# Slot attention and FP8 FFN on one core: where the output projection's products stand among a unit's other products

## The chip, the cores and the metric

The kernel runs on one core of a Trainium2 chip. Its time is the device time in microseconds (us) of that core; the number compared is the median of several runs. TensorE (PE in the profile, its weight loads PEld) multiplies, VectorE (DVE), ScalarE (ACT) and GpSimd (POOL) work on the products, and SyncE (SP) issues most of the DMAs.

## The reference: what is computed

Four sequences of 512 tokens with 512 features go through one layer. After a layer norm, attention with 16 heads and 64 slots per head reads and writes running states; after a second layer norm there is a feed-forward part whose weights are rounded to FP8. Cut to the attention (the recurrences run over the tokens):

```python
q, k, v, s = heads of h @ Wq, h @ Wk, h @ Wv, clip(h @ Ws, -32, 32)     # 64, 64, 128, 64 wide
z = cumlogsumexp(s);  g = exp(z_prev - z);  p = exp(s - z)
hk = hk * g + k (x) p;   ok = q . hk                # scores of the 64 slots
pv = softmax(ok)                                    # weights of the slots
hv = hv * g + p (x) v;   ov = pv . hv               # the read-out, 128 wide
o = ov * rsqrt(mean(ov**2) + eps) * g_norm * silu(h @ Wg)
x = x + o @ Wo                                      # the output projection
x = x + ffn(layernorm(x))
```

## The kernel before, in words

The 16 heads are taken two at a time (8 groups `g`) and the four sequences `b` in two pairs, which gives 32 units (g, b). Groups alternate: an even group also computes the values of the next odd one, so its unit is longer. Within a unit the 512 tokens stand in 4 blocks `n` of 128. The recurrences are turned into products: inside a block with a triangular mask (`diagonal_blocks`), and between blocks with sums of states (`states`, `add_up`).

The order of all engines is written out by hand: instructions stand on each engine's queue in the order in which Python calls them, and each engine works in that order. `attention` (L952) writes out one unit. It computes the unit X and, woven into it, the end of the unit before (`before`): normalising, gating, and the output projection `project_output` (L861), 4 blocks. A block's projection is six 128x512 products: four into the sum `ps_o` (parts 0 and 1 of the operands, two heads each) and two into `ps_o_m` (part 2). ACT then copies `ps_o` to `y` (L879), and `add_output` (L882) lets DVE subtract `ps_o_m` (L884) and POOL issue a DMA that adds `y` to the stream in DRAM (L885).

The second half of a unit, in which the change lies, runs thus on PE (L1051 to L1084):

- `slot_scores` ends with products into `ps_ok` (L731); DVE multiplies them into `okT` (L739).
- `value_states`: products into `ps_sv` (L636), which DVE adds up.
- `softmax`: four transposes of `okT` into `ps_okn` (L604); DVE takes the maxima `mx` (L746) and subtracts them (`ok`, L748); `softmax_exp` lets ACT take the exponential (L753).
- the projections of blocks 0 and 1.
- `slot_weights`: four transposes of `ok` into `ps_w`; DVE scales them into `wT` (L770).
- the projections of blocks 2 and 3; block 2's `ps_o_m` takes one of three shared banks, all other sums take turns in three "proj" banks.
- `weight_slot`: products of `eT` and `wT` into `ps_b` (L622); DVE masks them into two tiles `b` (L626), one for each head.
- `read_out`: products of `wT` with the states (L784), then of `b` with the values (L793), all into `ps_ov`; ACT squares, DVE reduces to `rs` (L804, L805), POOL takes the power (L808).

Two products of this stretch have row groups of their own: L622 and L784 use 64 rows each (64\*128 in the profile), two heads at a time; most others use 128 (128\*128).

The next unit then begins with 12 products each for s, k and q (L528, L551); DVE finishes `eT`, scales the output of the unit before (`og`, L813), runs the sum `z` (L688) and finishes `kT` (L555). `eT` is then transposed (`ps_e`), and `kT` (`ps_kn`), with the transposes of `og` (`ps_oT`) before it in odd groups.

Besides, a list `work` holds small pieces that have nothing to do with the unit at hand: splitting the weights of the groups to come (`w_...`, L256 on ACT, L263 to L268 on DVE) in the first 16 units, layer norms (`stats`, `mv`, `rstd`, `xn`, L342 to L349; `xs`, L378, L380), and rounding the FFN weights (`q`, `qw`, L471 to L485) in the last 16. `other`, `piece`, `small` take such pieces from the list at fixed places: between `softmax` and the projection of block 0 (L1054 to L1059), between the projections of blocks 2 and 3 (L1070), before `read_out` (L1076 to L1083), and in the next unit. `next_step` writes the transposes of a layer norm. `need("o")` empties the list up to the weights of the projection.

Of the kernel before, what the change touches and what calls it, by code (L numbers as in the profile page):

```python
# [37 lines left out]
F32 = mybir.dt.float32  # L38
# [6 lines left out]
P = 128  # L45
# [4 lines left out]
def kernel(  # L50
# [18 lines left out]
    nc = tc.nc  # L69

    B, T, D = x.shape
# [6 lines left out]
    HG = 2  # L78
# [15 lines left out]
    ps3 = ctx.enter_context(tc.tile_pool(name="ps3", bufs=3, space=bass.MemoryType.PSUM))  # L94
# [15 lines left out]
    def bank(name, n=None):  # L110
        if n is None:
            n = turn[0]
            turn[0] = (n + 1) % 3
        if n in held:
            held.pop(n)()
        return ps1.tile([P, 512], F32, tag=f"bank{n}", name=name)
# [47 lines left out]
    wt = {}  # L164
    split = {}
    work = []
# [3 lines left out]
    def other(count=None):  # L170
        for _ in range(count or pace[0]):
            if work:
                work.pop(0)[1]()

    def piece():

        while work:
            name, run = work.pop(0)
            run()
            if not name.endswith("_") and run is not scale_low:  # L180
                break

    def need(key):

        while any(name == key for name, _ in work):
            other(1)
# [4 lines left out]
    for g in range(NG):  # L191
# [3 lines left out]
        for nm in names:  # L195
            n = g if nm != "v" else 0 if g == 0 else (g + 1) // 2
# [5 lines left out]
    def fetch():  # L202
        if to_fetch:
            nm, g, part, chunks = to_fetch.pop(0)
            src, width = MATRICES[nm]
            tag = f"raw{fetched[0] % 2}"
            fetched[0] += 1
            w = one.tile([P, RAW], F32, tag=tag, name=f"raw_{nm}_{g}_{part}")[:, : chunks * width]
            if nm == "o":
                rows = src[g * HV : (g + 1) * HV, :]  # L210
            else:
                rows = src[part * chunks * P : (part + 1) * chunks * P, g * width : (g + 1) * width]
            nc.sync.dma_start(
                w.rearrange("p (c n) -> p c n", c=chunks), rows.rearrange("(c p) n -> p c n", p=P)
            )
            raw.setdefault((nm, g), []).append(w)
# [72 lines left out]
    def turned():  # L289

        return bool(work) and work[0][0][:3] == "xs_"

    def next_step():
        if steps:
            steps.pop(0)()
# [221 lines left out]
    class Projection:  # L517


        def __init__(self, nm, b, col0, name):  # L520
            self.nm, self.b, self.col0, self.name = nm, b, col0, name
# [131 lines left out]
    class Heads:  # L653


        def __init__(self, g, b):
            self.u, self.g, self.b = f"{g}_{b}", g, b
            self.v0 = g % 2 * HV
            self.sg = []
            self.y = {}  # L660

        def slots(self):

# [108 lines left out]
        def weight_slot(self):  # L772
            self.bb = diagonal_blocks(self.eT, self.wT, f"b_{self.u}")

        def read_out(self):


            po = [
                ps2.tile([P, NT, DV], F32, tag="acc", name=f"ps_ov_{self.u}_{h}") for h in range(HG)
            ]  # L780
            for n in range(1, NT):
                for h in range(HG):
                    rows = slice(h * M, (h + 1) * M)
                    nc.tensor.matmul(  # L784
                        po[h][:, n, :],
                        self.wT[rows, n * P : (n + 1) * P],
                        self.sv[rows, n - 1, :],
                        start=(n == 1),
                        stop=False,
                    )  # L790
            for h in range(HG):
                for n in range(NT):
                    nc.tensor.matmul(  # L793
                        po[h][:, n, :],
                        self.bb[h][:, n, :],
                        both_v[self.b][:, n, self.v0 + h * DV : self.v0 + (h + 1) * DV],
                        start=False,
                        stop=(n == NT - 1),
                    )
            self.og = one.tile([P, HG, NT, DV], F32, tag="og", name=f"og_{self.u}")  # L800
            rs = two.tile([P, HG, NT], F32, tag="rs", name=f"rs_{self.u}")
            for h in range(HG):
                nc.scalar.activation(self.og[:, h], po[h], AF.Square)  # L803
                nc.vector.tensor_reduce(rs[:, h, :], self.og[:, h], AX.X, ALU.add)  # L804
            nc.vector.scalar_tensor_tensor(  # L805
                rs, rs, 1.0 / DV, self.sm.rearrange("p (n h) -> p h n", h=HG), ALU.mult, ALU.add
            )
            nc.gpsimd.tensor_tensor(rs, rs, mhalf.rearrange("p (h n) -> p h n", h=HG), ALU.pow)  # L808
            self.po, self.rs = po, rs

        def scale_output(self):

# [45 lines left out]
            lo = self.oT[:, 1, h, :]  # L858
            nc.scalar.mul(lo, lo.bitcast(F32), 1.0 / DELTA)

        def project_output(self, n, in_bank=False):  # L861

            name = f"ps_o_{self.u}_{n}"
            p = ps3.tile([P, D], F32, tag="proj", name=name)
            m = bank(name + "_m") if in_bank else ps3.tile([P, D], F32, tag="proj", name=name + "_m")
            for dst, which in ((p, (0, 1)), (m, (2,))):
                for i in which:
                    for h in range(HG):
                        nc.tensor.matmul(  # L869
                            dst,  # L870
                            self.oT[:, i, h, n * P : (n + 1) * P],
                            wt["o"][:, i, h * D : (h + 1) * D],
                            start=(i == which[0] and h == 0),
                            stop=(i == which[-1] and h == HG - 1),
                        )
            if n == 0:
                self.y_all = one.tile([P, NT, D], F32, tag="y", name=f"y_{self.u}")
            y = self.y_all[:, n, :]
            nc.scalar.mul(y, p, 1.0 + DELTA)  # L879
            self.y[n] = y, m  # L880
# [6 lines left out]
    def exp_and_log():  # L887
        nc.scalar.preload_act_table_set("natural_log_exp_and_others")

    def first_unit():  # L890


        X = Heads(0, 0)

        parts = layernorm(0, 1, first=lambda: X.values(0))
        for nm in "skqv":
            load_matrix(nm, 0, True)
        for item in [item for item in work if item[0] in ("s_", "k_", "q_")]:
            work.remove(item)
            item[1]()  # L900
        X.values(1)
        for _ in range(5):
            piece()
        transposing = layernorm(1, 1)
        work.extend(parts())
        load_matrix("g", 0, True)
        other(2)
        X.slots()
        other(2)
        X.keys(X.running_sum)  # L910
        other(2)
        X.queries(None)
        X.turn_e()
        X.turn_k()
        other(2)
        X.values(2)
        other(2)
        X.key_states()
        X.inverse()
        X.values(3)  # L920
        fetch()
        fetch()
        load_matrix("o", 0, True)
        other(1)
        transposing()
        next_step()
        other(2)
        X.query_key()
        next_step()
        other(3)  # L930
        X.gate_main(0)
        X.slot_scores()
        X.value_states()
        next_step()
        X.softmax()
        X.softmax_exp()
        other(1)
        X.gate_main(1)
        X.slot_weights()
        next_step()  # L940
        X.gate_silu(0)
        X.gate_silu(1)
        exp_and_log()
        X.weight_slot()
        need("xs_1")
        X.softmax_sum()
        need("xs_0")
        piece()
        X.read_out()
        return X  # L950

    def attention(g, b, before, load, gated):  # L952
# [3 lines left out]
        X = Heads(g, b)  # L956
# [93 lines left out]
        exp_and_log()  # L1050
        X.slot_scores()  # L1051
        X.value_states()
        X.softmax()
        if even and b == 1 and not first and not turned():  # L1054
            piece()
        elif not turned():
            small()
        elif not even and b > 1:
            other(1)  # L1059
        need("o")  # L1060
        before.project_output(0)
        X.softmax_exp()
        before.add_output(0)
        before.project_output(1)
        X.slot_weights()
        before.add_output(1)
        next_step()
        before.project_output(2, True)
        before.add_output(2)
        small()  # L1070
        before.project_output(3)
        load("o")
        X.weight_slot()
        before.add_output(3)
        X.softmax_sum()
        if even and b == 1 and not first and not turned():  # L1076
# [3 lines left out]
        if even:  # L1080
            next_step()
            if turned():
                other(1)  # L1083
        X.read_out()  # L1084
        if not even and b < 2:
            next_step()
            if turned():
# [97 lines left out]
    with tc.manual_schedule(engines=EVERY):  # L1185
# [13 lines left out]
        before = first_unit()  # L1199
# [3 lines left out]
        for i, (g, b) in enumerate(units[1:], 1):  # L1203
# [53 lines left out]
            before = attention(g, b, before, load, gated)  # L1257
# [11 lines left out]
        for b in range(B):  # L1269
            need(f"xs_{b}")  # L1270
            for c in range(NFC):
                if c > 1:
                    other(2)
                h = ffn_hidden(b, c)
# [74 lines left out]
```

## Time and profile before

| | |
|---|---|
| median of 3 runs | 1456.88 us (1455.47 to 1457.69) |
| span of the profiled execution | 1454.5 us |
| mean granted TensorE clock | 0.999 |
| PE, busy | 1429.6 us (98%), 8875 matmuls |
| PEld, busy | 1178.9 us (81%) |
| DVE, busy | 1104.0 us (76%) |
| ACT, POOL, busy | 709.9 us (49%), 240.0 us (16%) |
| chain that ended last | PE 89%, DVE 7%, ACT 2%, issue 1% |

The profile's own execution spans 1454.5 us from its first to its last instruction; the median of the runs is 2.4 us above that. Rows of a timeline read: start, duration of the merged group, engine, line, operation, written tile <- read tiles, shape, count, and in brackets the idle time of the engine before the group with what ended it. PE's ends are modelled and overlap the next start, so the distance from start to start is the better measure.

### The profile page before, as it was taken

Reading aid. Unit: us, or ns where it says so; the run is one execution under the profiler, and the core shown is the slowest. Engines: PE = TensorE matmul, PEld = TensorE weight load, DVE = VectorE, ACT = ScalarE, POOL = GpSimd, SP = SyncE. Lnnn points to the kernel's source line nnn. Section 1 sums busy time; section 2 is a strip of 40 time slices with the busy share of each in tenths; the row PEclk is TensorE's granted clock in tenths of the full one; section 3 lists DMA queues with packets and bytes.
Section 4 is the critical chain, followed back from the end, with each engine's and each line's share of the span. In section 5 each row is a group of like instructions: output and inputs, shape, how many; then the busy total and the mean of one; then the engine's idle time right before and its main releaser. Section 6 shows DMA issues by size and latency. Waiting matters only on the chain.

```text
span 1454.5 us, 22772 instructions
## 1 busy us (share of the span) xinstructions
PE 1429.6 (98%) x8875; PEld 1178.9 (81%) x8875; DVE 1104.0 (76%) x1968; ACT 709.9 (49%) x1215; POOL 240.0 (16%) x271
## 2 busy tenths in 40 slices
PE   9999999999999999999999999999999999999998
PEld 4778888888888888888888888888888788888886
DVE  6888868976897689878888898898889863435333
ACT  4555555555665556554545554556445542222221
POOL 2012111211121122211211121111112111000000
PEclk9999999999999999999999999999999999999999
DMA  8274556565655474456546654666465562101000
GB/s 333 86 218 138 182 160 172 175 191 158 174 174 185 135 232 123 138 156 192 160 109 196 203 161 108 196 203 173 127 179 174 145 181 30 59 0 58 1 29 29
DMA packets 80859, 212.51 MB, mean 146 GB/s; under 512 B 6168, under 2 KB 35120, under 8 KB 75568
## 3 DMA queue, kind: packets, MB, share of 16 engines
q1 hardware_dynamic: 62224, 177.49, 33.1%
q0 software_dynamic: 18528, 33.58, 15.2%
q8 instruction: 70, 1.15, 0.3%
q14 instruction: 37, 0.30, 0.1%
HBM read 107.23 MB, written 108.00 MB: 148 GB/s over the span
## 4 chain that ended last, share of the span: by engine, by line
PE 89%; DVE 7%; ACT 2%; issue 1%; POOL 0%; DMA 0%; DVEq 0%; POOLq 0%
PE ps_o L869 8%; PE ps_g L528 8%; PE ps_v L587 7%; PE ps_fg L1097 6%; PE ps_fu L1097 6%; PE ps_ov L793 4%; PE ps_o_m L869 4%; PE ps_g_m L551 4%; PE ps_v_m L587 4%; PE ps_s L528 3%; PE ps_k L528 3%; PE ps_q L528 3%; PE ps_fd L1158 3%; PE ps_fe L1158 3%; PE ps_b L622 2%; PE ps_a L622 2%
## 5 line engine op out<-in xcount | busy, mean ns | idle before, releaser
L885 POOL DMA_DIRECT2D stream<-y x128 | 112.4, 884 | 476.3 <-DVE y L884 468.6
L869 PE MATMUL ps_o<-w_o,oT 128*128 128x512 f32 x512 | 145.2, 405 | 0.0
L528 PE MATMUL ps_g<-xs,w_g 128*128 128x512 f32 x496 | 125.2, 394 | 0.0
L587 PE MATMUL ps_v<-w_v,xs 128*128 128x512 f32 x480 | 122.3, 397 | 0.2 <-DVE qT L555 0.2
L1118 DVE SCALAR_TENSOR_TENSOR h<-ps_fu,scol,act 128x512 f32<-128x512 f32 x48 | 36.0, 750 | 111.5 <-PE ps_fu L1097 110.2
L879 ACT ACTIVATE y<-ps_o 128x512 f32<-128x512 f32 x128 | 76.5, 598 | 74.9 <-PE ps_o L869 74.9
L528 PEld LDWEIGHTS ps_g<-xs,w_g 128*128 128x128 f32 x496 | 91.7, 188 | 19.7
L869 PEld LDWEIGHTS ps_o<-w_o,oT 128*128 128x128 f32 x512 | 91.4, 188 | 17.4
L587 PEld LDWEIGHTS ps_v<-w_v,xs 128*128 128x128 f32 x480 | 87.7, 188 | 19.4 <-DVE qT L555 0.6
L713 POOL COPY sk_both<-sk 64x192 f32<-64x192 f32 x64 | 43.5, 679 | 343.4 <-DVE sk L649 341.5
L1097 PE MATMUL ps_fg<-xs,wf 128*128 128x512 f32 x384 | 95.6, 391 | 0.0
L884 DVE TENSOR_TENSOR y<-y,ps_o_m 128x512 f32<-128x512 f32 x128 | 87.2, 681 | 10.4 <-ACT y L879 9.8
L1097 PE MATMUL ps_fu<-xs,wf 128*128 128x512 f32 x384 | 94.8, 389 | 0.0
L595 ACT ACTIVATE v<-ps_v 128x512 f32<-128x512 f32 x60 | 35.9, 599 | 99.9 <-PE ps_v L587 99.9
L803 ACT ACTIVATE og<-ps_ov 128x512 f32<-128x512 f32 x64 | 38.1, 597 | 94.5 <-PE ps_ov L793 94.5
L1097 PEld LDWEIGHTS ps_fu<-xs,wf 128*128 128x128 f32 x384 | 72.1, 188 | 15.0
L1097 PEld LDWEIGHTS ps_fg<-xs,wf 128*128 128x128 f32 x384 | 71.6, 188 | 14.6
L869 PE MATMUL ps_o_m<-w_o,oT 128*128 128x512 f32 x256 | 79.4, 391 | 0.2 <-ACT y L879 0.2
L596 DVE TENSOR_TENSOR v<-v,ps_v_m 128x512 f32<-128x512 f32 x60 | 41.0, 684 | 48.6 <-PE ps_v_m L587 48.6
L1124 ACT CAST both<-h 128x512 fp32r<-128x512 f32 x48 | 29.8, 621 | 94.5 <-DVE h L1118 94.5
L1115 ACT ACTIVATE act<-ps_fg,scol 128x512 f32<-128x512 f32 x48 | 33.0, 688 | 87.7 <-PE ps_fg L1097 87.7
L533 ACT ACTIVATE sg<-ps_g 128x512 f32<-128x512 f32 x62 | 37.0, 596 | 71.4 <-PE ps_g L528 44.4
(171 smaller groups left out, 3327.0 us busy)
## 6 DMA issues: line engine op xcount, KB each, us to landing
stream<-y POOLq DMA_DIRECT2D x128, 256.0 KB, 6.3
split_v<-w_v SPq DMA_DIRECT2D x4, 3072.0 KB, 12.3
split_g<-w_g SPq DMA_DIRECT2D x8, 1536.0 KB, 7.6
split_o<-w_o SPq DMA_DIRECT2D x8, 1536.0 KB, 6.3
w_v<-split_v SPq DMA_DIRECT2D x4, 3072.0 KB, 16.3
w_g<-split_g SPq DMA_DIRECT2D x8, 1536.0 KB, 6.6
w_o<-split_o SPq DMA_DIRECT2D x8, 1536.0 KB, 9.5
rounded<-qw SPq DMA_DIRECT2D x36, 256.0 KB, 3.7
```

Source lines behind the costliest of these rows:

```text
L528: nc.tensor.matmul(self.p, products(self.nm, c, self.col0, i), xs[self.b][i][:, c, :], start=(i == 0 and c == 0), stop=(i == 1 and c == KC ...
L551: nc.tensor.matmul(self.m, products(self.nm, c, self.col0, 2), xs[self.b][2][:, c, :], start=(c == 0), stop=(c == KC - 1),)
L587: nc.tensor.matmul(dst, xs[b][i][:, c, n * P : (n + 1) * P], wt["v"][:, i, c * 2 * HV : (c + 1) * 2 * HV], start=(i == which[0] and c == 0 ...
L622: nc.tensor.matmul(pa[h][:, n, :], lT[rows, cols], rT[rows, cols], start=True, stop=True)
L713: nc.gpsimd.tensor_copy(sk_both[rows, :, h * M : (h + 1) * M], self.sk[rows])
L793: nc.tensor.matmul(po[h][:, n, :], self.bb[h][:, n, :], both_v[self.b][:, n, self.v0 + h * DV : self.v0 + (h + 1) * DV], start=False, stop ...
L869: nc.tensor.matmul(dst, self.oT[:, i, h, n * P : (n + 1) * P], wt["o"][:, i, h * D : (h + 1) * D], start=(i == which[0] and h == 0), stop= ...
L879: nc.scalar.mul(y, p, 1.0 + DELTA)
L884: nc.vector.tensor_tensor(y, y, m, ALU.subtract)
L885: nc.gpsimd.dma_start(stream[self.b][n * P : (n + 1) * P, :], y, accum_op=ALU.add)
L1097: nc.tensor.matmul(pp, w[:, c * P : (c + 1) * P], xs[b][k][:, c, :], start=(c == 0 and k == 0), stop=(c == KC - 1 and k == 1),)
L1158: nc.tensor.matmul(sums[n], parts[k][:, n * P : (n + 1) * P], fw[c][2], start=(c == 0 and k == 0), stop=(c == NFC - 1 and k == 1),)
```

## The change

The products of the projection get other places in the unit; what is computed stays. `project_output` can now emit a part of a block's six products (`count`) and go on later. `read_out` is cut in two: `read_states` (the products with the states) and `read_within` (the rest). In `attention`:

- two products of block 0 stand before the transposes of `softmax`, if no piece of the projection's weights is waiting;
- two products of block 2 stand before the transposes of `slot_weights`, its other four behind them;
- `weight_slot` stands before the projection of block 3, and that projection stands between `read_states` and `read_within`;
- the pieces of `work` that stood between `softmax` and block 0 stand behind `slot_weights`; the `small()` that stood between blocks 2 and 3 stands behind `weight_slot`.

```diff
-        def read_out(self):
+        def read_states(self):
-            po = [
+            self.po = po = [
...
+        def read_within(self):
+            po = self.po
...
-        def project_output(self, n, in_bank=False):
-            name = f"ps_o_{self.u}_{n}"
-            p = ps3.tile([P, D], F32, tag="proj", name=name)
-            m = bank(name + "_m") if in_bank else ps3.tile([P, D], F32, tag="proj", name=name + "_m")
-            for dst, which in ((p, (0, 1)), (m, (2,))):
...
+        def project_output(self, n, in_bank=False, count=None):
+            if n not in self.left:
+                name = f"ps_o_{self.u}_{n}"
+                p = ps3.tile([P, D], F32, tag="proj", name=name)
+                self.left[n] = [(p, i, h) for i in (0, 1) for h in range(HG)] + [
+                    (None, 2, h) for h in range(HG)
+                ]
+                self.sums[n] = [p, None]
+            p, m = self.sums[n]
+            for _ in range(count or len(self.left[n])):
+                dst, i, h = self.left[n].pop(0)
+                if dst is None:
+                    if m is None:
+                        name = f"ps_o_{self.u}_{n}_m"
+                        m = bank(name) if in_bank else ps3.tile([P, D], F32, tag="proj", name=name)
+                        self.sums[n][1] = m
+                    dst = m
+                nc.tensor.matmul(
+                    dst,
+                    self.oT[:, i, h, n * P : (n + 1) * P],
+                    wt["o"][:, i, h * D : (h + 1) * D],
+                    start=(i in (0, 2) and h == 0),
+                    stop=(i in (1, 2) and h == HG - 1),
+                )
+            if self.left[n]:
+                return
...
         X.value_states()
+        if not any(name[0] == "o" for name, _ in work):
+            before.project_output(0, count=2)
         X.softmax()
+        need("o")
+        before.project_output(0)
+        X.softmax_exp()
+        before.add_output(0)
+        before.project_output(1)
+        before.project_output(2, count=2)
+        X.slot_weights()
         if even and b == 1 and not first and not turned():
             piece()
         elif not turned():
             small()
         elif not even and b > 1:
             other(1)
-        need("o")
-        before.project_output(0)
-        X.softmax_exp()
-        before.add_output(0)
-        before.project_output(1)
-        X.slot_weights()
         before.add_output(1)
         next_step()
         before.project_output(2, True)
         before.add_output(2)
+        X.weight_slot()
         small()
+        X.read_states()
         before.project_output(3)
         load("o")
-        X.weight_slot()
         before.add_output(3)
         X.softmax_sum()
...
-        X.read_out()
+        X.read_within()
```

The first unit has no unit before it and keeps its order, and the last unit's projection stands in the feed-forward part, whole blocks at a time.

More of the change, by code (lines that the diff above doesn't have):

```diff
@@ L659, in __init__ @@
             self.sg = []
-            self.y = {}
+            self.y, self.left, self.sums = {}, {}, {}
         def slots(self):
@@ L808, in read_out @@
             nc.gpsimd.tensor_tensor(rs, rs, mhalf.rearrange("p (h n) -> p h n", h=HG), ALU.pow)
-            self.po, self.rs = po, rs
+            self.rs = rs
         def scale_output(self):
@@ L859, in low_output @@
             nc.scalar.mul(lo, lo.bitcast(F32), 1.0 / DELTA)
-        def project_output(self, n, in_bank=False):
-            name = f"ps_o_{self.u}_{n}"
-            p = ps3.tile([P, D], F32, tag="proj", name=name)
-            m = bank(name + "_m") if in_bank else ps3.tile([P, D], F32, tag="proj", name=name + "_m")
-            for dst, which in ((p, (0, 1)), (m, (2,))):
[L867 to L875, printed above, removed]
+        def project_output(self, n, in_bank=False, count=None):
[24 more added lines that the diff above has]
+                return
             if n == 0:
@@ L1069, in attention @@
         before.add_output(2)
+        X.weight_slot()
         small()
+        X.read_states()
         before.project_output(3)
         load("o")
-        X.weight_slot()
         before.add_output(3)
@@ L1083, in attention @@
                 other(1)
-        X.read_out()
+        X.read_within()
         if not even and b < 2:
```

## The prediction

> **What bounds the kernel now.** First the page: PE is busy 98% and carries 89% of the chain, so the time is PE's products plus what PE waits for.
>
> ```profile
> PE 1429.6 (98%) x8875; PEld 1178.9 (81%) x8875; DVE 1104.0 (76%) x1968; ACT 709.9 (49%) x1215; POOL 240.0 (16%) x271
> ...
> PE 89%; DVE 7%; ACT 2%; issue 1%; POOL 0%; DMA 0%; DVEq 0%; POOLq 0%
> ```
>
> Then the list of PE's waits. It hides the steady ones: it shows 1.5 us for `ps_okn`, but the view of that tile sums 14.8 us of idle (PE and PEld together) ended by `okT`, and the view of `ps_ov` 10.6 us ended by `b`. So the timeline has to be read, here of an odd unit, its PE and PEld, then its DVE.
>
> ```profile
> 436.17 1.09 PE L731 MATMUL ps_ok<-a,e 128*64 128x128 f32 x16
> 437.10 0.82 PE L636 MATMUL ps_sv<-v,e 128*64 128x128 f32 x12
> 438.06 0.66 PE L604 MATMUL ps_okn<-ident,okT 128*128 128x128 f32 x4
> 438.47 1.18 PE L869 MATMUL ps_o<-w_o,oT 128*128 128x512 f32 x4
> ...
> 441.33 0.60 PE L604 MATMUL ps_w<-ident,ok 128*128 128x128 f32 x4
> 441.73 1.19 PE L869 MATMUL ps_o<-w_o,oT 128*128 128x512 f32 x4
> 443.21 1.09 PE L869 MATMUL ps_o<-w_o,oT 128*128 128x512 f32 x4
> 444.69 1.16 PE L622 MATMUL ps_b<-wT,eT 64*128 64x128 f32 x16
> 445.68 0.84 PE L784 MATMUL ps_ov<-sv,wT 64*128 64x128 f32 x12
> 446.63 2.05 PE L793 MATMUL ps_ov<-v,b 128*128 128x128 f32 x16
> ```
>
> ```profile
> 438.06 0.42 PEld L604 LDWEIGHTS ps_okn<-ident,okT 128*128 128x128 f32 x4 [0.38 <-DVE okT L739]
> 446.62 0.74 PEld L793 LDWEIGHTS ps_ov<-v,b 128*128 128x128 f32 x6 [0.30 <-DVE b L626]
> ```
>
> See two waits per unit: the 12 records of `ps_sv` hold PE for 0.96 us up to `ps_okn`, where the 16 in front took 0.93; and the 12 of L784 for 0.95, up to L793. Both are ended by DVE, as PEld's brackets say, and both come in every unit but the first, 31 times. They are the places that the change fills. The same unit on DVE:
>
> ```profile
> 438.83 0.68 DVE L746 TENSOR_REDUCE mx<-ps_okn 128x8 f32<-128x512 f32 x1
> 440.15 0.68 DVE L263 TENSOR_TENSOR w_s<-raw_s,w_s 128x512 fp32r<-128x512 f32 x1
> 442.08 0.68 DVE L770 TENSOR_TENSOR wT<-ps_w,rzT 128x512 f32<-128x512 f32 x1
> 443.59 0.69 DVE L884 TENSOR_TENSOR y<-y,ps_o_m 128x512 f32<-128x512 f32 x1 [0.23 <-ACT y L879]
> 445.88 1.29 DVE L626 TENSOR_TENSOR b<-ps_b,tri 128x512 f32<-128x512 f32 x2 [0.27 <-PE ps_b L622]
> 449.35 0.69 DVE L804 TENSOR_REDUCE rs<-og 128x4 f32<-128x512 f32 x1 [0.19 <-ACT og L803]
> ```
>
> See that DVE has three short waits only from `mx` on: it is nearly full here, and what it has to do is fixed. The same queue must then deliver `kT` for the next unit's transposes. In a late unit the two stand so:
>
> ```profile
> 1076.47 0.68 DVE L555 TENSOR_TENSOR kT<-kT,ps_k_m 128x512 f32<-128x512 f32 x1
> ...
> 1077.70 0.60 PE L604 MATMUL ps_kn<-ident,kT 128*128 128x128 f32 x4
> ```
>
> `kT` ends at 1077.15, 0.55 us ahead of its reader.
>
> **PE's gain per unit.** No product is added; I lay the new order out from the start of `ps_sv`, 437.10. Rates from start to start: pairs of 64-wide products 0.11, twelve projection products behind transposes 2.86 (438.47 to 441.33), six 1.48, two 0.45, four transposes 0.36 unwaited. `ps_sv` takes 0.70; two products of block 0, with the entry behind 64-wide ones, 0.57: `ps_okn` at 438.37, after `okT` (437.31+0.69=438.00). Transposes to 438.73; twelve products to 441.59; `ps_w` to 441.95; four products 1.02 and the entry to 64-row ones 0.09: `ps_b` at 443.06. From there 0.99 (as 444.69 to 445.68), 0.76 for the states' six pairs and the way back to 128 rows, 1.49 for block 3: L793 at 446.30, and the next unit at 448.00 (0.10 less, since its first product does not wait) instead of 448.43. The gain is 0.43 us. Bounds: PE's own idle, 0.14+0.11=0.25, and PEld's, 0.38+0.30=0.68; I stay with the layout between them.
>
> The new waits in that layout. Block 2's first product takes the bank of block 0's `ps_o_m`, which DVE frees by the first `y` subtraction: `mx` 439.02 (0.19 later), `ok` 0.72 and `y` 0.61 later, done 441.02; the product's weights load 0.2 before its start at 441.14. Late by some 0.05: gain 0.40. `wT` can start 0.31 after the last transpose has (as `okT` does after the last `ps_ok`), 442.28 to 442.97, ahead of `ps_b` at 443.06 to 443.1. `b`: behind it DVE has the piece moved here (0.60, 0.72), `y`, `y` (0.61, 0.60), so `b` 445.41 to 446.10 against 446.30. Three margins of 0.1 to 0.2 us; below them 0.1 more lateness costs 0.1 a unit. ACT is in time: `y` of block 0 can start at 439.4 now that the `w_s` copy (0.63) no longer precedes it, and is done 0.3 before DVE wants it.
>
> The two split blocks add borders between transposes and products. Row: `ps_w` starts 0.45 after two products begin, products 0.40 after the transposes, no dearer than inside a group; I price a border at nothing (upper bound 0.02). [...]
>
> **What the moved pieces cost.** DVE used the time in which it now waits for `ps_w` for a piece. In the unit above, the queue has done the same list 1.50 us later (`wT` 0.18 later and 1.32 of piece behind it), less the waits that close, 0.23+0.27+0.19: 0.8 us late at `rs` and, the queue being full up to it, at `kT`, while PE comes 0.40 earlier. `ps_kn` then waits 0.8+0.40+0.05 (the first transpose's extra, 329 against 273 ns) less its slack. In the late unit pieces L478, L479 are shorter (1.06), the lateness 0.76, the slack 0.55: wait 0.7, unit 0.3 slower. Where DVE waits for POOL's `rs` before `og`, closing the wait before `eT` gives nothing. The slack `kT` to `ps_kn`, the closing waits and the piece, read so in every unit (numbered from 0):
>
> - 12 units keep 0.40: without a piece here (4, 8, 12, 16), with slack 1.96 (7, 11), with wide waits before `b` or `eT` (17, 18, 21, 26, 29), and the last, 31: 4.8 us.
> - 3 and 15: `okn` waits 0.6 longer, two whole products fit: 0.63 each, 1.3.
> - 6, 10, 20, 22 to 25, 27: slack 0.5 to 1.07, 0.08 to 0.24 left: 1.2.
> - 5, 9, 13, 19, 28: slack 0.55 to 0.94, lateness 0.8 to 0.9: -0.31, -0.33, -0.07, -0.31, -0.35: -1.4.
> - 1, 2, 14, 30 already wait at `ps_kn` (up to 1.15 us) for a chain that starts at `rs`: PE's gain is lost and DVE's shift remains. 1 has no piece before `wT`, `rs` comes 0.7 earlier: +0.7. 2: 0.8 late; 30: 1.51 less 0.67, 0.84 late; 14, without any wait to close, 1.55 late: -3.2.
>
> Sum: 4.8+1.3+1.2-1.4+0.7-3.2 = 3.4 us faster. Against the profiled execution: span 1454.5 to 1451.1; the median lies 2.4 above, 1453.5.
>
> At nothing I price: the split DMAs and raw loads of the moved pieces, which go on SP 2.5 us later (they land in 3.1 to 6.5 us; the `w_q` load of the unit above is wanted 5.5 us after its new issue; a late one would hold a later piece, 1 us in some of the nine units that have such a piece here); `load("o")` 1.7 us later (lands in 9.5, read 30 us on); POOL's stream DMA of block 3, about 1 us later and still 1 us ahead of POOL's power; k's bank, freed by block 3's `y` at 448.7 and wanted at 450.9. Each cover that fails puts its own lateness on PE once a unit.
>
> **The rivals.**
> 1. *The lateness is absorbed.* If `kT` is not later, each unit keeps 0.40, 12.4 us and 0.5 at 3 and 15: 1444. For it: DVE idles 24% overall. Against: not one wait between `rs` and `kT` in the late units.
> 2. *The waits before `b` do not close (slower).* If DVE, now reaching `y` and `b` in another order, still waits 0.7 there, the lateness is 1.5 instead of 0.8. Price: 0.7 in nine units (5, 6, 9, 10, 13, 19, 22, 25, 28) and about 0.4 in eight more, 9.5 us in all: 1463; half of it 1458. It decides from 0.25 us of extra lateness a unit, which eats the 3.4. For it: the margins above. Against: both blocks' sums are complete before DVE arrives.
> 3. *The waits only move.* Blocks 0 and 2 wait for their bank as long as `okn` did: the unit keeps 0.14 of the 0.40. The sum then reads 1.7+0.8+0.9-1.4+0.7-3.2 = 0.5 us slower, 1457.4. For it: block 2 starts 0.05 us from its bank's release. Against: a wait of 0.26 there needs DVE 0.2 later than its rows.
>
> **Chances and range.** Forecast 0.55 (1450 to 1456.5), rival 1 0.12, rival 2 0.23, rival 3 0.10. The range reaches towards 1 and to half of 2: 1446.5 to 1459.5. About 0.2% (2.9 us) is what a measurement can tell from no change: faster 0.36+0.12 = 0.48, same 0.19+0.10 = 0.29, slower 0.23.
>
> **What would show it.** `ps_sv` to the first product 0.70, no PEld idle before `ps_okn` and L793, 448.0 instead of 448.4 within the unit; DVE idle 1.2 us before `wT`, none before `b`; and PE waits for `kT` at `ps_kn` in about 13 more units, 0.1 to 0.7 us each. Wrong if L793 or `ps_b` waits for DVE in most units (slower), or if `ps_kn` never waits (1444).

## The result, and the profile after

The changed kernel takes 1458.04 us (median of 21 runs, 1456.78 to 1460.88), the kernel before 1456.22 (21 runs, 1455.06 to 1457.69). The ratio is 1.0015, with a 95% interval of 1.0009 to 1.0021: it is slower by 0.15%, where 0.2% faster was forecast. The profiled execution took 1456.78 us, its span is 1455.1, 0.6 longer than before's. Of the 21 runs it is the fastest; in twelve of the others the mean granted clock is lower than its 0.998 (0.994 to 0.997), and no profile shows where.

The page shows next to nothing of it (first its busy times, then the chain):

```profile
PE 1430.3 (98%) x8875; PEld 1176.3 (81%) x8875; DVE 1101.0 (76%) x1968; ACT 705.8 (49%) x1215; POOL 242.3 (17%) x271
...
PE 86%; DVE 7%; ACT 3%; issue 2%; POOL 1%; DMA 0%; SPq 0%; POOLq 0%; DVEq 0%
```

The list of PE's waits does (us in total, times, longest). Before, its line for `kT` read 2.1 us in 2, and it had no line for `ps_b` and `y`:

```profile
PE ps_kn L604 <- DVE kT L555: 4.7, 7, 1.8
PE ps_b L622 <- DVE y L900: 4.6, 2, 2.7
PE ps_xn L361 <- DVE xn L349: 4.6, 5, 2.1
...
PE ps_kn L604 <- DVE xs L378: 1.2, 2, 0.6
PE ps_oT L604 <- ACT e L700: 0.8, 4, 0.2
```

4.6 us in two waits is more than the whole gain that was forecast. They stand in units 14 and 30. First, though, the ordinary unit: the same one that the prediction reads, unit 11, on PE.

```profile
435.56 0.82 PE L636 MATMUL ps_sv<-v,e 128*64 128x128 f32 x12
436.31 0.73 PE L883 MATMUL ps_o<-w_o,oT 128*128 128x512 f32 x2
436.88 0.60 PE L604 MATMUL ps_okn<-ident,okT 128*128 128x128 f32 x4
437.23 0.71 PE L883 MATMUL ps_o<-w_o,oT 128*128 128x512 f32 x2
...
440.15 0.60 PE L604 MATMUL ps_w<-ident,ok 128*128 128x128 f32 x4
...
441.61 1.16 PE L622 MATMUL ps_b<-wT,eT 64*128 64x128 f32 x16
442.61 0.84 PE L784 MATMUL ps_ov<-sv,wT 64*128 64x128 f32 x12
...
444.87 1.95 PE L797 MATMUL ps_ov<-v,b 128*128 128x128 f32 x16
446.57 2.07 PE L528 MATMUL ps_s<-xs,w_s 128*128 128x512 f32 x8
```

From `ps_sv` to the next unit it now takes 446.57-435.56 = 11.01 us, where it took 448.43-437.10 = 11.33: 0.32 less. The waits before `ps_okn` and for `b` are closed, as the change was laid out. DVE in the same unit:

```profile
440.78 0.69 DVE L770 TENSOR_TENSOR wT<-ps_w,rzT 128x512 f32<-128x512 f32 x1 [1.26 <-PE ps_w L604]
...
443.91 1.28 DVE L626 TENSOR_TENSOR b<-ps_b,tri 128x512 f32<-128x512 f32 x2
...
453.56 0.66 DVE L555 TENSOR_TENSOR kT<-kT,ps_k_m 128x512 f32<-128x512 f32 x1
```

It idles 1.26 us before `wT`, not at all before `b`, and `kT` comes 18.00 us after the unit's `ps_sv` (453.56-435.56), where it came after 17.44 (454.54-437.10): 0.56 late. Before's row:

```profile
454.54 0.66 DVE L555 TENSOR_TENSOR kT<-kT,ps_k_m 128x512 f32<-128x512 f32 x1
```

In the late unit of the prediction, 28, the lateness is 0.63 (1075.38-1055.93 against 1076.47-1057.65), and there PE waits:

```profile
1076.11 0.66 PE L604 MATMUL ps_kn<-ident,kT 128*128 128x128 f32 x4 [0.31 <-DVE kT L555]
```

Now unit 14, PE:

```profile
552.72 0.60 PE L361 MATMUL ps_xn<-ident,xn 128*128 128x128 f32 x4
...
553.62 0.62 PE L883 MATMUL ps_o_m<-w_o,oT 128*128 128x512 f32 x2
554.17 0.48 PE L622 MATMUL ps_b<-wT,eT 64*128 64x128 f32 x2
557.34 1.04 PE L622 MATMUL ps_b<-wT,eT 64*128 64x128 f32 x13 [2.68 <-DVE y L900]
...
559.62 2.07 PE L883 MATMUL ps_o<-w_o,oT 128*128 128x512 f32 x4
```

and DVE:

```profile
553.52 0.68 DVE L342 BATCH_NORM_STATS2 stats<-x 128x6 f32<-128x512 f32 x1
...
554.98 0.68 DVE L900 TENSOR_TENSOR y<-y,ps_o_m 128x512 f32<-128x512 f32 x1
555.58 0.69 DVE L342 BATCH_NORM_STATS2 stats<-x 128x6 f32<-128x512 f32 x1
...
556.60 0.69 DVE L900 TENSOR_TENSOR y<-y,ps_o_m 128x512 f32<-128x512 f32 x1
```

In this unit the transposes `ps_xn` of a layer norm take one of the three shared banks. `ps_b` needs two, and the second one it gets is that of block 2's `ps_o_m`. Before, block 3 stood between block 2 and `ps_b`, so PE came 1.5 us later (six products). Now `ps_b` follows block 2 at once, and its third product waits until DVE has subtracted that very sum: the `y` at 556.60, queued behind a piece that was moved there and behind a second one (`stats`, `mv`, `rstd`) that stood there before too. Unit 30 is built alike (1.93 us). The same places before, on PE and on DVE:

```profile
556.00 0.62 PE L869 MATMUL ps_o_m<-w_o,oT 128*128 128x512 f32 x2
...
557.90 1.18 PE L622 MATMUL ps_b<-wT,eT 64*128 64x128 f32 x15
```

```profile
557.29 0.69 DVE L884 TENSOR_TENSOR y<-y,ps_o_m 128x512 f32<-128x512 f32 x1
```

Behind the changed kernel's wait, the table of the windows (start and end, length, busy time and instructions of PE, PEld, DVE, ACT, POOL; then the granted TensorE clock, the DMA share and GB/s):

```profile
554.70:557.30 2.60, 0.00 (x0) 0.00 (x0) 2.52 (x6) 0.00 (x0) 2.07 (x3) 1.00 0.20 34
557.40:558.40 1.00, 1.00 (x18) 1.00 (x20) 0.08 (x1) 0.00 (x0) 0.86 (x2) 1.00 1.13 80
558.50:561.80 3.30, 3.30 (x16) 2.69 (x14) 2.86 (x5) 0.07 (x1) 0.00 (x0) 0.50 0.91 132
```

The clock falls to half for these 3.3 us (3.41 by its records), and block 3's first four products span 1.87 us (559.62 to 561.49) where they took 1.04 in unit 11 (443.37 to 444.41).

### The profile page after: what moved, and what is told of

Read it like the earlier page. It is cut to its first block, busy times and chain, and to the rows that moved or that the text cites. A ratio compares the mean times of both kernels' runs of the same rounds, so it can differ in the third digit from the quotient of the medians.

```text
span 1455.1 us, 22778 instructions
## 1 busy us (share of the span) xinstructions
PE 1430.3 (98%) x8875; PEld 1176.3 (81%) x8875; DVE 1101.0 (76%) x1968; ACT 705.8 (49%) x1215; POOL 242.3 (17%) x271
## 3 DMA queue, kind: packets, MB, share of 16 engines
q8 instruction: 70, 1.15, 0.3%
## 4 chain that ended last, share of the span: by engine, by line
PE 86%; DVE 7%; ACT 3%; issue 2%; POOL 1%; DMA 0%; SPq 0%; POOLq 0%; DVEq 0%
PE ps_o L883 8%; PE ps_g L528 8%; PE ps_v L587 8%; PE ps_fg L1118 6%; PE ps_fu L1118 6%; PE ps_g_m L551 4%; PE ps_v_m L587 4%; PE ps_o_m L883 4%; PE ps_fd L1179 3%; PE ps_ov L797 3%; PE ps_fe L1179 3%; PE ps_s L528 3%; PE ps_k L528 3%; PE ps_q L528 2%; PE ps_a L622 2%; PE ps_ok L731 2%
## 5 line engine op out<-in xcount | busy, mean ns | idle before, releaser
L883 PE MATMUL ps_o<-w_o,oT 128*128 128x512 f32 x512 | 163.3, 421 | 0.0
L883 PEld LDWEIGHTS ps_o<-w_o,oT 128*128 128x128 f32 x512 | 84.8, 190 | 25.2 <-DVE y L900 7.0
L812 POOL TENSOR_TENSOR rs<-rs,mhalf 128x8 f32<-128x8 f32 x32 | 58.8, 1839 | 78.8 <-DVE rs L809 54.6
```

Source lines behind the costliest of these rows:

```text
L883: nc.tensor.matmul(dst, self.oT[:, i, h, n * P : (n + 1) * P], wt["o"][:, i, h * D : (h + 1) * D], start=(i in (0, 2) and h == 0), stop=(i ...
```

## The experiments

The kernel before, run on the same chip beside the first four, took 1455.78 us (19 runs); beside the last four 1455.56 (9 runs). Ratios are to those.

**1. Another bank for block 2's second sum.** The changed kernel, but in units with `ps_xn` (`held`) that sum takes one of the "proj" banks, so that a shared bank is free for `ps_b`:

```diff
-        before.project_output(2, True)
+        before.project_output(2, not held)
```

> The changed kernel, but in the two units (numbers 14 and 30) in which a layer norm's transposes hold a shared bank, block 2's third sum goes into a proj bank instead, so that ps_b finds two free banks. Bank theory (the forecast's missing loss is ps_b waiting for block 2's y in these two units, 2.7 and 1.9 us, with a stretch of half TensorE clock behind the longer wait): both waits at ps_b and the stretch of half clock are gone; 2 to 2.5 us come back in unit 14 and 1 to 1.5 in unit 30 (what is left there is kT, which the forecast had), so 3 to 4.5 us below the changed kernel and 1.5 to 2.5 below before. Rival, lateness theory (the loss is DVE's lateness at ps_kn over many units): less than 1 us below the changed kernel, so no better than before.

Measured: 1454.04 us (1452.38 to 1455.62, 11 runs), ratio 0.9986 (0.9977 to 0.9995). The waits for the bank are gone from the list, and no half clock is left behind them (mean granted clock 0.999, against the changed kernel's 0.998); instead PE waits at `ps_kn`, in unit 14 1.88 us:

```profile
PE ps_kn L604 <- DVE kT L555: 4.5, 6, 1.8
PE ps_kn L604 <- DVE xs L378: 3.2, 2, 1.9
```

Unit 14 now loses 1.57 us and unit 30 0.65, against before. That is the chain from `rs` to `ps_kn` that the prediction priced (1.55 and 0.84): in unit 14 it takes 9.95 us before and here (563.63 to 573.58, 562.52 to 572.47), and `rs` starts 1.59 us later behind the unit's `ps_sv` (15.26 against 13.67). One line, which touches two of 32 units, turns the result from slower to faster: the bank is the cause of the sign.

**2. The read-out part alone.** The kernel before, with `weight_slot` ahead of block 3 and block 3 between `read_states` and `read_within`:

```diff
+        X.weight_slot()
         small()
+        X.read_states()
         before.project_output(3)
         load("o")
-        X.weight_slot()
...
-        X.read_out()
+        X.read_within()
```

> The kernel before with the read-out part alone: weight_slot ahead of block 3, block 3 between the read-out's halves; blocks 0 and 2 and the pieces ahead of block 0 as before. The wait before L793 is filled: 0.17 us a unit, 5 us in 31. Bank theory: ps_b waits for block 2's y in units 14 and 30 here too, but shorter, since fewer pieces stand ahead of that y on DVE: about 1.2 and 0.7 us; in all some 3 us below before. Lateness theory: the pieces ahead of wT have not moved, so ps_kn waits no longer than before, and nothing of the 5 us is lost.

Measured: 1451.74 us (1451.39 to 1453.18, 7 runs), ratio 0.9975 (0.9964 to 0.9986); about 0.20 us a unit. The waits for the bank come with this part:

```profile
PE ps_kn L604 <- DVE kT L555: 2.2, 2, 1.3
PE ps_kn L604 <- DVE xs L378: 1.6, 2, 1.0
PE ps_b L622 <- DVE y L888: 1.6, 2, 1.0
```

They are shorter than in the changed kernel (1.02 and 0.54 against 2.68 and 1.93), since fewer pieces stand ahead of `y`; and `kT` is no later than before. Units 14 and 30 lose 1.15 and 0.85 us; every unit from 3 on besides these gains, 0.17 to 0.23.

**3. The front part alone.** The changed kernel with `weight_slot` and the read-out where they were: products ahead of both groups of transposes, pieces behind `slot_weights`.

```diff
-        X.weight_slot()
         small()
-        X.read_states()
         before.project_output(3)
         load("o")
+        X.weight_slot()
...
+        X.read_states()
         X.read_within()
```

> The changed kernel with weight_slot and the read-out as before: only blocks 0 and 2 ahead of the transposes and the pieces behind ps_w. The wait before ps_okn is filled: 0.15 us a unit, 4.6 us in 31, and the wait before L793 stays. Bank theory: block 3's 1.4 us stand between block 2 and ps_b and cover most of the bank's wait (about 1.3 and 0.5 us stay), the waits at ps_kn cost 3 to 5 us as in the changed kernel: within 1.5 us of before. Lateness theory: as slow as the changed kernel, 1 to 2 us above before.

Measured: 1468.46 us (1467.8 to 1468.88, 4 runs), ratio 1.0085 (1.0071 to 1.0098), far from what was expected. The list names it in one line, and unit 11's DVE shows why:

```profile
PE ps_ov L797 <- DVE b L626: 18.1, 23, 1.2
```

```profile
446.54 0.69 DVE L770 TENSOR_TENSOR wT<-ps_w,rzT 128x512 f32<-128x512 f32 x1 [1.26 <-PE ps_w L604]
447.14 0.68 DVE L263 TENSOR_TENSOR w_s<-raw_s,w_s 128x512 fp32r<-128x512 f32 x1
...
449.67 0.68 DVE L263 TENSOR_TENSOR w_k<-raw_k,w_k 128x512 fp32r<-128x512 f32 x1
...
450.99 1.28 DVE L626 TENSOR_TENSOR b<-ps_b,tri 128x512 f32<-128x512 f32 x2
```

Both pieces now stand between `wT` and `b`, and nothing on PE lies between `ps_ov`'s products with the states and those with `b`. In the whole change the second piece is behind `b` and block 3 covers the first. The two halves do not add: alone -4.0 and +12.7 us, together +1.8, or -1.7 with the bank mended.

**4. The small piece ahead of `kT` moved behind it** (on top of experiment 1):

```diff
         def running_sum():
             before.scale_other()
             X.running_sum()
-            if not first:
-                small()

         X.keys(running_sum)
+        if not first:
+            small()
```

> The first of these kernels, and the piece that stood between the running sum z and kT on DVE stands behind kT, so that kT comes up to 1.3 us earlier. Bank theory and the forecast's step on kT: the waits of ps_kn for kT (4.7 us in seven units of the changed kernel, 3.1 of them in units 1 and 2) go, and with the bank's waits gone too the kernel is 2.5 to 5 us below the first one, 5 to 7 below before. If the waits at ps_kn are not DVE's lateness but come from PE's side, nothing changes against the first one. New risk: qT now stands behind the piece; in units 1 and 2 that piece waits for ACT and a may wait 0.5 us for qT.

Measured: 1451.42 us (1450.26 to 1453.2, 7 runs), ratio 0.9972 (0.9961 to 0.9983), 2.6 better than experiment 1 and 4.4 below before, where 5 to 7 was expected. The line for `kT` has left the list; part of it has moved on:

```profile
PE ps_oT L604 <- ACT e L700: 3.0, 5, 0.9
PE ps_kn L604 <- DVE xs L378: 3.0, 2, 1.8
```

So the waits at `ps_kn` for `kT` are DVE's queue, as the prediction had it, and the next in line is ACT's `e`: units 1, 2, 19 and 28 gain 1.0, 0.9, 0.5 and 0.5 us against experiment 1, while units 5 and 9 wait for `e` instead and gain nothing. In this profile, unlike experiment 1's, the clock falls to half in units 14 and 30 (mean granted clock 0.996 against 0.999; see the last section).

**5. Experiment 2 with the bank mended** (`before.project_output(2, not held)` there too).

> The kernel before with the read-out part alone (weight_slot ahead of block 3, block 3 between the states' products and the rest), and with block 2's second sum in a proj bank instead of a shared one in units 14 and 30. The same without the other bank gave 1451.7 with waits for that bank of 1.02 and 0.54 us. Theory (units 14 and 30 are set by DVE's chain from rs to kT and xs, the wait for the bank lies beside it): the two waits at ps_b go and come back at ps_kn; 1451.2 to 1451.7, 0.5 us faster at most. Rival (the wait for the bank is PE time of its own): the whole 1.6 us, 1450.1.

Measured: 1451.49 us (1449.6 to 1451.78, 5 runs), ratio 0.9967 (0.9954 to 0.9979): 0.25 from experiment 2, nothing that can be told by the medians. The traces decide for the rival all the same. Unit 14 lost 1.15 us in experiment 2 and loses 0.02 here: its wait of 1.02 us for the bank, with what this delayed, was time of its own and did not lie beside the wait for `xs` (0.97 there, 1.32 here). Unit 30 hides its share: it lost 0.85 there and loses 1.44 here, since here a stretch at half clock follows its wait of 2.07 us for `xn`, which experiment 2's trace has without such a stretch (mean granted clock 0.998 here, 0.999 there). The five times fit this: 1449.6 and 1449.9 us at a mean granted clock of 0.999, 1451.5 to 1451.8 at 0.997 or 0.998. An estimate from the first two and from experiment 2's times at 0.999 (1451.4 to 1452.0) is that changing the bank is worth 1.5 to 2.4 us.

**6. Experiment 5, and two products of block 0 ahead of the transposes of `softmax`**; pieces at their old place, block 2 whole.

```diff
         X.value_states()
+        if not any(name[0] == "o" for name, _ in work):
+            before.project_output(0, count=2)
         X.softmax()
```

> The run above, and two products of block 0 ahead of the transposes of softmax; the pieces stay where they were, block 2 is whole. Theory (the wait before ps_okn is PE time that two products fill, and DVE, whose list keeps its order, is no later at kT): 0.15 to 0.20 us a unit in 30 units, 4.5 to 6 us faster than without, 1445 to 1447, ps_okn without waits, ps_kn waits as before (2.2 us). Rival (the wait only moves: mx starts 0.19 later, so the piece behind it, y and wT do, and ps_b or block 1's bank waits as long): within 1 us of the run above, 1450.5 to 1452, with waits of 0.1 to 0.2 at ps_b or at the projection in most units.

Measured: 1450.11 us (1448.38 to 1450.7, 5 runs), ratio 0.9958 (0.9945 to 0.997), 1.4 better than experiment 5: a third of what was expected, 0.06 us a unit (0.26 against 0.20). `ps_okn` no longer waits, but PEld does, one step on (here in unit 11):

```profile
437.85 0.42 PEld L604 LDWEIGHTS ps_w<-ident,ok 128*128 128x128 f32 x4 [0.29 <-ACT ok L753]
```

The transposes come 0.36 us later than without the two products, so `mx`, `ok` and its exponential do, and `ps_w` waits for it. The list of PE's waits doesn't hold this wait either. Here lies the use of block 2's split: its two products fill this place (in unit 11 of the changed kernel PEld does not wait before `ps_w`).

**7. Experiment 6 with the small piece behind `kT`** (the edit of 4).

> The run above, and the small piece that stood ahead of kT on DVE behind it. Theory (units 1 and 2 wait 1.27 and 0.97 us at ps_kn for kT, and the piece ahead of kT is about 0.6 to 1.1 of it): 1.5 to 2.2 us faster than the run above. Rival (the waits move on to ps_oT, which waits for ACT's e, and to later readers of the piece): within 0.5 us of it, with 1 to 2 us of waits at ps_oT.

Measured: 1447.55 us (1446.14 to 1447.78, 5 runs), ratio 0.9942 (0.9928 to 0.9956), 2.6 better than 6. This is the best kernel of the study, 0.6% faster than the kernel before. `kT` has left the list, and little takes its place; the gain lies in units 1 and 2 (1.02 and 0.97 us), which wait for `kT` in the kernel before too:

```profile
PE ps_kn L604 <- DVE xs L378: 2.2, 2, 1.6
...
PE ps_oT L604 <- ACT e L700: 0.3, 1, 0.3
```

**8. The changed kernel with the bank mended and the pieces back** between `softmax` and block 0.

```diff
         X.softmax()
+        if even and b == 1 and not first and not turned():
+            piece()
+        elif not turned():
+            small()
+        elif not even and b > 1:
+            other(1)
         need("o")
...
         X.slot_weights()
-        if even and b == 1 and not first and not turned():
-            piece()
-        elif not turned():
-            small()
-        elif not even and b > 1:
-            other(1)
```

> The changed kernel with block 2's second sum in a proj bank in units 14 and 30 (that alone gave 1454.0), and the pieces back at their place between softmax and the projection of block 0. Theory (the split of block 2 needs the pieces moved: its first product takes the bank that DVE's first y subtraction frees, and that stands behind the piece): waits of about 1.0 us at ps_o for y in each of some 27 units with a piece, 25 to 30 us; ps_kn waits for kT fall back from 4.5 to about 2 us: 1472 to 1480. Rival (the bank is free in time, the move of the pieces only makes kT late): 1449 to 1451.

Measured: 1461.68 us (1460.3 to 1461.97, 5 runs), ratio 1.0039 (1.0026 to 1.0051), 7.6 slower than experiment 1. The sign is the theory's, the size a third, and the releaser another one:

```profile
PE ps_o L883 <- ACT y L895: 8.1, 25, 0.3
...
PE ps_kn L604 <- DVE kT L555: 2.3, 2, 1.3
```

```profile
438.47 0.63 ACT L256 ACTIVATE w_s<-raw_s 128x512 fp32r<-128x512 f32 x1
439.00 0.58 ACT L895 ACTIVATE y<-ps_o 128x512 f32<-128x512 f32 x1
439.85 0.63 ACT L753 ACTIVATE ok<-ok 128x512 f32<-128x512 f32 x1 [0.26 <-DVE ok L748]
440.38 0.58 ACT L895 ACTIVATE y<-ps_o 128x512 f32<-128x512 f32 x1
```

Block 2's first product (at 441.01) waits 0.33 us for the end of ACT's second `y` copy, which stands behind the piece's `w_s` copy and the exponential. It starts before DVE's first `y` subtraction does (441.05), so its bank cannot be the one that this frees. By the releasers the pool has dealt the banks anew: in the changed kernel block 2's first sum takes the bank of block 0's `ps_o_m`, as the prediction said; with `y` behind the piece it gets that of block 1's `ps_o` instead, which ACT frees. That is the part of the 25 us that did not come. The waits for `kT` fall back to the 2 us of before, which confirms what the moved pieces do to DVE. With block 2 split the pieces have to go; without the split (experiment 7) they can stay, and `kT` stays in time.

## Why the prediction was wrong

Unit by unit (from one start of `ps_sv` to the next, unit 31 up to the feed-forward part's first product, in the two traces), gains in us:

| units | forecast | measured |
|---|---|---|
| 4, 7, 8, 11, 12, 16, 17, 18, 21, 26, 29, 31 | 4.8 | 3.4 |
| 3, 15 | 1.3 | 1.2 |
| 6, 10, 20, 22 to 25, 27 | 1.2 | 2.2 |
| 5, 9, 13, 19, 28 | -1.4 | -1.7 |
| 1 and 2 | -0.1 | -0.2 |
| 14 | -1.55 | -3.8 |
| 30 | -0.84 | -2.2 |
| sum | 3.4 | -1.1 |

Of the 4.5 us that the sums differ, units 14 and 30 make 3.6. The spans differ by less than 1.1 us because the changed kernel's trace is 0.9 us ahead at its first `ps_sv` (43.90 against 44.77) and loses 0.4 behind unit 31. That units 1 and 2 come out right together is luck: 0.29 and -0.52 were measured, 0.7 and -0.8 forecast.

**The step that failed** is the one on the new waits "in that layout". It went through the banks of an ordinary unit and took the sum of units 14 and 30 from DVE's lateness alone. It listed `okT`, `wT`, `b` and the "proj" bank, and never asked which bank `ps_b` gets, though it is known of the kernel before that block 2's second sum takes a shared bank, and its trace shows `ps_xn` between `ps_w` and block 2 in unit 14 (at 554.63). A product moved up by a whole block comes that much nearer to the release of its bank: `ps_b` waits 2.68 and 1.93 us for `y`, and the two units lose 3.8 and 2.2 us where 1.55 and 0.84 were forecast. Experiment 1 undoes this alone, and units 14 and 30 then lose 1.57 and 0.65, close to the forecast. The second thing not seen is the half clock behind the longer wait (0.50 for 3.41 us): no row of before has one ahead of the kernel's end.

**The gain of an ordinary unit** was 0.40; it measured 0.27 to 0.37 in most. The layout can be checked from unit 11's rows: `ps_sv` to the first product 0.75 (forecast 0.70), to `ps_okn` 1.32 (1.27), to `ps_w` 4.59 (4.49), to `ps_b` 6.05 (5.96), to L797 9.31 (9.20), to the next unit 11.01 (10.90). So the entry from 64-wide products cost 0.05 more than the row that was taken for it, and the twelve products between the transposes 0.05 more. The wait for `y`'s bank, which the forecast added at 0.05, is in the second (PEld idles 0.22 us before block 2's first load, ended by `y`); how much of it the borders make, priced at nothing with an upper bound of 0.02, the rows do not separate. The margins of `wT` and `b` held.

**DVE's lateness** was right in kind and forecast somewhat too large: 0.8 forecast, 0.56 in unit 11, 0.63 in unit 28 (0.76 forecast). PE waits for `kT` in five more units (0.18 to 0.44 us), not in about 13. Of the five units that were to lose, four lost (0.63, 0.67, 0.19, 0.22) and one broke even; the eight with little slack kept 0.15 to 0.37 instead of 0.08 to 0.24. That some of PE's waits would come back at `ps_kn` for `kT` is shown by experiment 4, which removes them, and by experiment 8, in which they fall back with the pieces. Units 18 and 21 lost their gain, and units 5 and 9 some more, at `ps_oT` to ACT's `e` (0.17 to 0.25 us), which the prediction did not name.

**Weight loads.** In unit 11 after, two products at 439.64 are followed by the transposes `ps_w`, whose loads begin at 439.92, before the second product's modelled end at 440.31 and before their own start at 440.15; the four new borders cost at most about 0.1 us a unit together (what unit 11 is longer than the layout), so the prediction's price of nothing for a border held to within that.

**The rivals.** Lateness absorbed (1444): no, `ps_kn` waits. Waits before `b` not closing: no, in no unit of the changed kernel's list, but experiment 3 shows that this holds only because block 3 lies between. Waits only moving (1457.4): nearest in time, for another reason; its mechanism shows in experiment 8 (block 2 waits 0.33 us for its bank where the pieces are not moved), and experiment 6 shows the like at `ps_w`. The split DMAs and `load("o")` cost nothing that the waits show.

## What to carry to other kernels

Before a product is moved up, write down for every unit that differs from the ordinary one which bank each of its tiles takes and which instruction frees it: two units of 32 turned this change's sign. Filling a wait in a serial chain moves the next wait of that chain nearer; the fill is worth what the next place can also fill, and the work that is put aside for it has to be costed on the queue where it lands. Of a change in several parts, try the parts alone: here the read-out part, block 0's first products and one small piece moved behind `kT` were better than the whole, which also splits block 2. Read a small difference of medians unit by unit as well: experiment 5's 0.25 us hid two effects of over 1 us each.

## What the runs showed of the hardware

Behind the wait of 2.68 us the granted clock was 0.50 for 3.41 us (by the trace's clock records, from 558.47), beginning 1.1 us after PE had started again. Behind the 1.93 us wait of unit 30 it stayed at 1.00; in experiment 4's profile it fell twice, behind waits of 1.76 and 2.07 us, each time for 3.4 us (mean granted clock of that profile 0.996). The wait of 2.07 us (`ps_xn` in unit 30) stands in all ten traces, and a half-clock stretch follows it in three (experiments 3, 4 and 5, at a mean granted clock of 0.997, 0.996 and 0.998; experiments 1 and 2 have the wait at 0.999). So it does not follow from the wait's length alone.

In the 3.41 us ahead of the changed kernel's stretch (555.06 to 558.47) PE was busy, by its modelled ends, for 1.13 us. What sets such a stretch off was not shown.

What a stretch costs can be read where the same products run with and without one. Behind the wait of 2.07 us the first twelve products of `ps_g` and `ps_g_m` take 4.43 us in experiment 4 (1151.16 to 1155.59) and 2.83 us in experiment 1 (1153.07 to 1155.90): 1.60 us. Units 14 and 30 lose 3.13 and 2.25 us in experiment 4, against 1.57 and 0.65 in experiment 1. In the changed kernel's unit 14 the shares of the wait and of the half clock in the 2.23 us that it loses beyond experiment 1 cannot be told apart, since the later wait at `ps_kn` shrinks from 1.88 to 0.54 us.
